# A graph network on one core: reordering the first chunks and the last blocks of a hand-written schedule

## The chip, the core and the metric

The kernel runs on one core of a Trainium2 chip. The core has five engines that run side by side, each through its own list of instructions in order: TensorE (PE, matrix products; its weight loads are a second row, PEld), VectorE (DVE), ScalarE (ACT), GpSimd (POOL) and SyncE (SP), which here only issues DMAs. The metric is the device time of one execution in microseconds (us), as the median of several runs.

## The reference

There are 128 graphs of 64 nodes with 128 features (`x`), and an adjacency matrix per graph (`adj`), ones on the diagonal and about one further entry in eight. One layer of message passing is computed:

```
pair[i, j]  = concat(x[i], x[j])
message     = mlp(pair; msg weights)                 # for each pair i, j
agg[i]      = sum over j of adj[i, j] * message[i, j]
out[i]      = x[i] + mlp(concat(x[i], agg[i]); upd weights)

mlp(v): h = layernorm(relu(v @ w0 + b0)) ; h = layernorm(relu(h @ w1 + b1)) ; h @ w2 + b2
```

All is float32. Messages are needed only where `adj` is one, so the kernel computes only those edges.

## The kernel before, in words

**Tiles.** Two graphs make a pair p (64 pairs), and each graph's edges fill at most 640 slots. Two pairs make a quad q (32 quads), which is 20 tiles of 128 edges. Four tiles are a chunk (160 chunks, five to a quad). Four pairs make a block b of nodes (16 blocks, ten chunks each).

**The way of an edge chunk.** For each pair, a table of one-hot columns `S` selects for every edge slot its two node rows; POOL, ACT and DVE build its halves (`node_rows`, `marks`, `compare`), and SP's DMAs stack them (`stack`). `rows` multiplies the turned `x` with the two halves of the first weight, `rows_hi` (ACT) and `rows_lo` (DVE) take the PSUM bank out as a high and a low part (`abh`, `abl`). `layer0` (L535) multiplies these with `S` into bank `hps` and ACT makes `h` (L538). `stats0` turns `h` on PE (L544) and DVE takes its statistics (L548). `var0_of` makes the variance of a quad (five operations on POOL; for the last quad on DVE), `root_of` its root on ACT (L255), split into a high and a low part (L562, L563), `turn_root` (L568) and `root_out` turn it into rows (`sdT`). `layer1` multiplies `h` with the centred second weight (L605), after a product of `sdT` with the bias table `b1t` (L602) or after ACT has seeded the bank (`seed`, L593); ACT makes `y` (L608), `stats1` its statistics on DVE (L615). `var1_step`, `root1_of` and `inverse_of` make one over the second deviation, `weights` (L678) scales a one-hot of destinations by it, and `reduce` (L691) sums the edges into nodes on PE: 20 products for two pairs, the scatter of a quad.

**The node update.** For each block, `Unit` holds the chain: `sums_out` copies the scatter's bank, `turn`, `turn_out` and `layer` go through three products, with relu and statistics on DVE (`layer_out`), variance, root, `upd_shift`, and `finish` (L791), which scales, adds the residual `xo` (POOL, L730) and issues the output DMA. `bias0` (DVE, L724) makes `m0`, the bias of its first product. The last block is split in two units of two pairs.

**The order.** Nothing is scheduled by a planner. Each step is entered by hand in `plan` under a chunk number and a place with `at(n, place, function, ...)`. For each chunk n the loop at the end runs the places in this order: `a`, `m`, layer 1 of chunk n - 8, `b`, layer 0, statistics 0, `k`, statistics 1, then `x`, `x1`, `x2`, `e0`, `e1`, `e`. A step's instructions go to their engines in that order, and an engine that waits holds all that stands behind it. PSUM has eight banks, each in a pool of one buffer: `mu` (`ubank`), `ma` (`abank`), `mk`, `hps`, `hT`, two `z`, `ys`.

**The head.** The steps for the first three chunks are written out ahead of the loop, with `keep_busy(k)`, which issues k products of a constant into a bank that nothing reads. During chunks 1 to 10 the loop also derives weights (`derivation`: products such as L180 in bank `mu` or a `z` bank, emptied by ACT or DVE), and `bias_table` and `bias_part` make `b1t` on POOL (L645 to L655). `odd_weights` (L427, L428) checks on DVE that `adj` holds only zeros and ones.

## Time and profile before

| | |
|---|---|
| median of 6 runs | 572.17 us (570.7 to 574.49) |
| the profiled execution, its own time | 572.43 us |
| its span | 570.7 us |
| PE busy | 549.1 us (96%) |
| DVE busy | 482.9 us (85%) |
| ACT busy | 480.8 us (84%) |
| POOL busy | 353.1 us (62%) |
| mean granted clock of PE | 0.989 |

The profile is one execution. Its span is counted from the first to the last instruction; the time of the execution is 1.73 us more. Busy times are sums over the whole span and say little about a stage: PE is busy through the body, so the edges of the span are read in windows of a few us and in the timeline. "PEclk" is the clock that PE was granted, 1.00 being full speed. In a timeline row the bracket gives how long the engine had been idle before, and which instruction ended that; a row with x4 merges four instructions that follow one another.

### The profile page before, as it was taken

To read this page: it belongs to the slowest core of one execution; us is meant where nothing else is said; L and a number is where in the kernel's file an instruction comes from. 1 tells how busy PE (TensorE), PEld (TensorE's weight loads), DVE (VectorE), ACT (ScalarE), POOL (GpSimd) and SP (SyncE) were. 2 spreads that over 40 slices of the span, in tenths; PEclk is the share of its full clock that TensorE was granted. 3 is DMA by queue.
4 is the path that set the end of the run, shared out by engine and by line. 5 is a ranking of instruction groups with operands and counts; after the bars stand their busy time and mean duration, and the time that the engine had idled before them with its cause. 6 is when DMAs were issued, how large, how long until landed. Compare 5 with 4: busy or idle time off the path is not lost. (4 is left out here: it accounts for less than half of the span.)

```text
span 570.7 us, 15800 instructions
## 1 busy us (share of the span) xinstructions
PE 549.1 (96%) x5325; PEld 514.8 (90%) x5325; DVE 482.9 (85%) x1944; ACT 480.8 (84%) x1153; POOL 353.1 (62%) x911
## 2 busy tenths in 40 slices
PE   8799899999999999999999999999999999989894
PEld 7587889999999999999999999999999999979883
DVE  6758788998989899898989899898989989885685
ACT  6778889998989899898989989898989989885533
POOL 3624566766757676675767676675767666545452
PEclk9889999999999999999999999999999999998999
DMA  4454747454564645655556545647454546432101
GB/s 103 121 127 114 136 104 132 107 132 109 107 155 105 142 92 143 112 118 127 126 130 113 141 108 132 106 111 153 112 143 84 131 113 108 113 94 28 39 20 42
DMA packets 90770, 63.23 MB, mean 111 GB/s; under 512 B 57398, under 2 KB 74812, under 8 KB 90684
## 3 DMA queue, kind: packets, MB, share of 16 engines
q1 hardware_dynamic: 90396, 62.03, 49.3%
q8 instruction: 44, 0.72, 0.6%
q14 instruction: 42, 0.34, 0.2%
q10 hardware_dynamic: 288, 0.13, 0.1%
HBM read 6.82 MB, written 4.19 MB: 19 GB/s over the span
## 5 line engine op out<-in xcount | busy, mean ns | idle before, releaser
L605 PE MATMUL z<-w1c,h 128*128 128x128 f32 x1280 | 172.8, 278 | 0.0
L548 DVE BATCH_NORM_STATS2 st<-hT 128x6 f32<-128x128 f32 x640 | 140.9, 282 | 32.1 <-PE hT L544 32.0
L605 PEld LDWEIGHTS z<-w1c,h 128*128 128x128 f32 x1280 | 161.0, 192 | 7.6 <-issue 5.1
L593 ACT ACTIVATE z<-b1b,m_sd 128x128 f32<-128x128 f32 x416 | 154.3, 371 | 10.4
L615 DVE BATCH_NORM_STATS2 st<-y 128x6 f32<-128x128 f32 x640 | 137.5, 277 | 2.8 <-ACT y L608 1.4
L608 ACT ACTIVATE y<-z 128x512 f32<-128x512 f32 x160 | 94.3, 590 | 22.3 <-PE z L605 20.6
L538 ACT ACTIVATE h<-hps,b0c 128x512 f32<-128x512 f32 x160 | 109.3, 683 | 2.2 <-PE hps L535 2.2
L544 PE MATMUL hT<-ident,h 128*128 128x128 f32 x640 | 97.9, 276 | 1.8 <-DVE st L548 1.6
L678 POOL TENSOR_TENSOR w<-oh,m_q 128x320 f32<-128x320 f16 x126 | 92.1, 743 | 9.9 <-PE hT L544 5.3
L535 PE MATMUL hps<-s,abl 128*128 128x512 f32 (+3 forms) x256 | 92.2, 372 | 2.0 <-ACT h L538 1.5
L544 PEld LDWEIGHTS hT<-ident,h 128*128 128x128 f32 x640 | 75.4, 141 | 13.9 <-DVE st L548 4.6
L535 PE MATMUL hps<-s,abh 128*128 128x512 f32 (+3 forms) x256 | 78.7, 326 | 0.0
L691 PE MATMUL ys<-y,w 128*64 128x128 f32 x1280 | 76.9, 275 | 0.0
L691 PEld LDWEIGHTS ys<-y,w 128*64 128x64 f32 x1280 | 69.2, 137 | 4.2 <-issue 3.6
L245 POOL TENSOR_TENSOR m_d<-st 128x20 f32<-128x20 f32 x62 | 16.4, 265 | 80.7 <-DVE st L548 69.0
L517 DVE TENSOR_TENSOR j<-mk,cmpt 128x320 fp32r<-128x320 f32 x124 | 58.7, 474 | 1.5 <-PE mk L509 1.5
L493 POOL CAST i<-tp 128x640 fp32r<-128x640 f16 x58 | 41.7, 719 | 25.2 <-ACT y L608 9.0
L478 ACT ACTIVATE d<-slot,mid 128x640 f16<-128x640 f16 x64 | 52.8, 824 | 0.0
L535 PEld LDWEIGHTS hps<-s,abl 128*128 128x128 f32 x256 | 49.3, 193 | 3.4 <-ACT h L538 2.3
L535 PEld LDWEIGHTS hps<-s,abh 128*128 128x128 f32 x256 | 49.5, 193 | 0.0
L469 DVE TENSOR_TENSOR abl<-mu,abh 128x512 fp32r<-128x512 f32 (+1 forms) x33 | 22.0, 668 | 30.3 <-ACT abh L463 30.2
L509 PE MATMUL mk<-tp,posall 128*128 128x320 f16 x126 | 38.0, 302 | 0.1
(227 smaller groups left out, 980.5 us busy)
## 6 DMA issues: line engine op xcount, KB each, us to landing
s<-i SPq DMA_DIRECT2D x124, 160.0 KB, 2.6
s<-j SPq DMA_DIRECT2D x124, 160.0 KB, 2.6
xn<-in_x_dram SPq DMA_DIRECT2D x15, 256.0 KB, 3.7
out_dram<-uo SPq DMA_DIRECT2D x15, 256.0 KB, 2.4
an<-in_adj_dram SPq DMA_DIRECT2D x16, 128.0 KB, 2.7
oh<-tp SPq DMA_TRANSPOSE x64, 3.4
xn<-in_x_dram SPq DMA_DIRECT2D x2, 128.0 KB
out_dram<-uo SPq DMA_DIRECT2D x2, 128.0 KB, 2.7
```

The costliest lines, as they stand in the source:

```text
L478: nc.scalar.activation(D[p], slot, AF.Abs, bias=blocks[b]["mid"][:, q:q + 1], scale=-1.0)
L517: nc.vector.tensor_tensor(JR[p][:, c], MK.pop((p, k))[:, 0:HC], cmpt[:, c], op=ALU.is_equal)
L535: nc.tensor.matmul(ps[:, c:c + w], lhsT=ab[:, g % 4, :], rhs=s, start=(k == 0), stop=(k == 1))
L538: nc.scalar.activation(H[n], ps, AF.Relu, bias=b0c)
L544: nc.tensor.transpose(ps[:, t, :], H[n][:, t * P:(t + 1) * P], ident)
L548: nc.vector.bn_stats(ST0[q][:, CH * c + t, :], ps[:, t, :])
L593: nc.scalar.activation(Z[n][:, t, :], W["b1b"], AF.Copy, scale=SR[q][:, k:k + 1])
L605: nc.tensor.matmul(ps[:, t, :], lhsT=h[:, t * P:(t + 1) * P], rhs=W["w1c"], start=False, stop=True, skip_group_check=True)
L608: nc.scalar.activation(Y[n], ps, AF.Relu)
L615: nc.vector.bn_stats(ST1[q][:, CH * c + t, :], Y[n][:, t, :])
L678: (nc.vector if p == NP - 2 else nc.gpsimd).tensor_tensor(WT[p][:, :, g, :], OH[p][:, :, g * N:(g + 1) * N], Q[q][:, k:k + TG].unsqueeze(2 ...
L691: nc.tensor.matmul(YS[b][g * N:(g + 1) * N, k, :], lhsT=w[:, t, g, :], rhs=y, start=(t == 0), stop=(t == TG - 1))
```

## The change

In the head, quad 0's variance moves in the order so that it stands ahead of `bias_table` on POOL. The rows of the second half of block 0 get bank `ma` in place of `mu`. Nine products of `keep_busy` are added at chunks 2 to 5. One cast and one distance (`node_rows(4)`, `distance(5)`) move behind the relu of their chunk on ACT. `odd_weights(0)` moves from chunk 18 to chunk 9. The first tiles of `adj` and `x` come from the pools that the later blocks use, and the loads of `adj` are issued six chunks later.

At the end, quad 31's variance (`var0_of`) runs in a new place `s`, ahead of layer 1 of its chunk, and the root and its turn one step earlier; the split of the root (L563) goes from DVE to POOL. The variances on DVE take one operation fewer, and two fewer where the first variance is folded in. The scatter of quad 29, the third last, goes from chunk 162 to chunk 167, behind the last layer 1; the copy of its sums follows it; quad 30's scatter takes bank `mk`. The buffers of `y` go from 12 to 15. `bias0` and `residual` of the last block come earlier, `finish` of block 13 later.

```diff
+    blkp = ctx.enter_context(tc.tile_pool(name="blk", bufs=3))
+    an0 = [blkp.tile([P, PB, N], F32, name="an", bufs=3) for b in range(2)]
+    xn0 = [blkp.tile([P, PB, C], F32, name="xn", bufs=5) for b in range(2)]
...
-    def square_sum(stp, st, n, name, eng=nc.gpsimd):
+    def square_sum(stp, st, n, name, eng=nc.gpsimd, m20=None):
...
-        eng.tensor_tensor(d, d, d, op=ALU.mult)
-        eng.tensor_scalar(d, d, C / 4.0, None, op0=ALU.mult)
+        if eng is nc.vector:
+            if m20 is not None:
+                eng.scalar_tensor_tensor(s, m20, EPS, s, op0=ALU.mult, op1=ALU.add)
+            eng.scalar_tensor_tensor(d, d, C / 4.0, d, op0=ALU.mult, op1=ALU.mult)
+        else:
+            eng.tensor_tensor(d, d, d, op=ALU.mult)
+            eng.tensor_scalar(d, d, C / 4.0, None, op0=ALU.mult)
...
     def var1_of(stp, st, m20, n, name, eng=nc.gpsimd):
+        if eng is nc.vector:
+            return square_sum(stp, st, n, name, eng, m20)
...
-        yp = es.enter_context(tc.tile_pool(name="yp", bufs=12))
+        yp = es.enter_context(tc.tile_pool(name="yp", bufs=15))
...
-            ps = blk["ab_ps", half] if k0 else ubank()
+            ps = blk["ab_ps", half] if k0 else abank() if (b, half) == (0, 1) else ubank()
...
-            eng_of(q).tensor_tensor(SH[q][:, 2:4, :], sdb, SH[q][:, 0:2, :].bitcast(F32),
+            nc.gpsimd.tensor_tensor(SH[q][:, 2:4, :], sdb, SH[q][:, 0:2, :].bitcast(F32),
...
-            if k == 0 or (b == NB - 1 and k == PB // 2):
+            if b == NB - 1 and k == 0:
+                YS[b] = ps_k.tile([P, 512], F32, name="mk").rearrange("p (k c) -> p k c", k=PB)
+            elif k == 0 or (b == NB - 1 and k == PB // 2):
                 YS[b] = ps_y.tile([P, PB, C], F32, name="ys")
...
-        LAST = ((1, 2, 3, 3, 4, 5, 6, 6, 8, 9, 10, 11, 11, 11, 12),
-                (0, 5, 6, 6, 7, 7, 8, 8, 8, 9, 9, 10, 10, 10, 11),
+        LAST = ((1, 2, 3, 3, 4, 5, 6, 6, 8, 9, 10, 11, 12, 11, 15),
+                (5, 5, 6, 6, 7, 7, 8, 8, 8, 9, 9, 10, 10, 10, 11),
...
-                at(max(o - 25, 0), "a", load_adj, b)
+                at(max(o - 19, 0), "a", load_adj, b)
...
-            for the last block: NCHK + L1 + 1, LAST[3], 1, 1 and NCHK + L1 - 1, LAST[2], 3, 3
+            for the last block: NCHK + L1 + 1, LAST[3], -5, 1 and NCHK + L1 - 1, LAST[2], -4, 3
-                at(n + m0_at, "m", bias0, u)
+                at(n + m0_at, "e" if b == NB - 1 else "m", bias0, u)
-                at(n + t[14], "m", finish, u)
+                at(n + t[14], "e" if b == NB - 3 else "m", finish, u)
...
-                    at(max(n - 7, p - 2), "a", distance, p)
+                    at(max(n - 7, p - 2), "x" if p == PB + 1 else "a", distance, p)
-                at(n - 5, "a", node_rows, p)
+                at(n - 5, "x" if p == PB else "a", node_rows, p)
...
-                wait = h + 2 if q == NQ - 3 else h + 1 if q == NQ - 2 else 2 + (2 * h + g + 1) // 2
+                wait = 3 if q == NQ - 3 else 2 if q == NQ - 2 else 2 + (2 * h + g + 1) // 2
-            at(NCHK + L1 + 1 if last else q * QC + SC - (q >= NQ - 3), "x1", reduce, p)
+            at(*((NCHK + L1 - 1, "x") if q == NQ - 3 else
+                 (NCHK + L1 + 1 if last else q * QC + SC - (q == NQ - 2), "x1")), reduce, p)
...
-            at(n, "e0", var0_of, q)
-            at(*((n, "e1") if last else (n + 1, "b")), root_of, q)
-            at(*((n + 2, "b") if last else (n + 1 if q else QC + 1, "x")), turn_root, q)
-            at(n + 2 if q else QC + 2, "x" if last else "a", root_out, q)
+            at(3 if q == 0 else n, "s" if last else "x" if q == 0 else "e0", var0_of, q)
+            at(*((n, "e0") if last else (n + 1, "b")), root_of, q)
+            at(*((n + 1, "x1") if last else (n + 1 if q else QC + 1, "x")), turn_root, q)
+            at(n + 2 if q else QC + 2, "a", root_out, q)
-            wait = 0 if last else 1 if q == NQ - 2 else 2
-            at(end + wait, "a", root1_of, q)
-            at(end + wait, "m", inverse_of, q)
+            wait = 0 if last else 2
+            at(end + wait, "x" if q == NQ - 2 else "a", root1_of, q)
+            at(end + wait, "x" if q == NQ - 2 else "m", inverse_of, q)
...
-        at(18, "m", odd_weights, 0)
+        at(9, "m", odd_weights, 0)
-        at(3, "b", bias_table)
+        at(3, "e", bias_table)
+        for n, k in ((2, 2), (3, 3), (4, 2), (5, 2)):
+            at(n, "e", keep_busy, k)
...
+            run(n, "s")
             if 0 <= n - L1 < NCHK:
                 layer1(n - L1)
```

The two lines on the last block's units stand for two longer lines in which only those numbers change.

## The prediction

> **What bounds the kernel now.** I read the page's slices first, then the busy time of short windows where they dip, then the timeline there.

> ```profile
> PE   8799899999999999999999999999999999989894
> PEclk9889999999999999999999999999999999998999
> ```

> TensorE (PE) is at nine tenths or more from about 60 to 510 us, so the body is PE's own work. Only the two ends, which the change edits, can give time back. The chain of waits is of no use here (two instructions), so I follow the timeline. Windows of the head (columns: length, busy us and count of PE, PEld, DVE, ACT, POOL, then granted clock, DMA share, GB/s):

> ```profile
> 22.00:24.00 2.00, 0.59 (x9) 0.35 (x6) 1.27 (x4) 0.58 (x1) 1.92 (x6) 1.00 0.67 163
> 24.00:26.00 2.00, 2.00 (x10) 1.33 (x10) 0.53 (x3) 1.15 (x4) 1.15 (x5) 0.82 0.73 176
> 26.00:28.00 2.00, 0.87 (x5) 0.58 (x4) 1.91 (x3) 2.00 (x6) 2.00 (x2) 0.50 0.27 60
> 30.00:32.00 2.00, 2.00 (x9) 1.57 (x7) 1.28 (x5) 1.22 (x4) 1.19 (x2) 0.50 0.02 4
> 32.00:34.00 2.00, 2.00 (x16) 1.78 (x15) 0.68 (x4) 1.06 (x3) 0.00 (x0) 0.98 0.68 163
> ```

> PE idles 1.4 us, and then runs at half clock: from 25.3 us (0.82 over 2 us is 0.72 us at half) to 32.1 us, 6.8 us in all. The timeline of the head (start, length, what; in brackets the idle time before it and who ended it):

> ```profile
> 22.93 0.45 POOL L649 TENSOR_TENSOR b1mix<-b1mix,b1lo 128x128 f32<-128x128 f32 x1
> 23.06 0.69 DVE L469 TENSOR_TENSOR abl<-mu,abh 128x512 fp32r<-128x512 f32 x1 [0.72 <-ACT abh L463]
> 23.35 0.25 POOL L245 TENSOR_TENSOR m_d<-st 128x20 f32<-128x20 f32 x1
> 23.81 0.49 PE L180 MATMUL mu<-wg,mean_m 128*128 128x128 f32 x2 [1.41 <-DVE abl L469]
> 24.82 0.31 ACT L255 ACTIVATE m_sd<-m,eps_c 128x20 f32<-128x20 f32 x1 [1.79 <-POOL m L249]
> 27.09 0.68 ACT L538 ACTIVATE h<-hps,b0c 128x512 f32<-128x512 f32 x1
> 27.82 0.48 PE L535 MATMUL hps<-s,abl 128*128 128x128 f32 x1 [1.13 <-ACT h L538]
> ```

> Two waits. A weight product (L180) needs bank mu, which the rows of the second half hold until DVE has emptied it. And ACT's root (L255) waits for POOL, whose variance stands behind the bias table's four operations; the relu of chunk 5 (L538) is queued behind that root, a cast and a distance, and PE waits for it.

> The end:

> ```profile
> 534.70 0.31 ACT L255 ACTIVATE m_sd<-m,eps_c 128x20 f32<-128x20 f32 x1 [2.13 <-DVE m L249]
> 535.56 0.31 PE L568 MATMUL ma<-ident,sh 128*80 128x128 f32 x1 [0.48 <-DVE sh L563]
> 535.80 2.40 PE L691 MATMUL ys<-y,w 128*64 128x128 f32 x40
> 538.13 0.51 PE L602 MATMUL z<-b1t,sdT 80*128 80x512 f32 x1
> 550.19 2.54 DVE L724 SCALAR_TENSOR_TENSOR m<-c2u,deg,ub0b 128x128 f32<-128x128 f32 x4
> 551.05 2.40 PE L691 MATMUL ys<-y,w 128*64 128x128 f32 x40
> 553.50 0.37 ACT L717 COPY ysum<-ys 128x256 f32<-128x256 f32 x1 [4.26 <-PE ys L691]
> 565.09 0.30 ACT L269 ACTIVATE um_sq<-um_v,eps_c 128x2 f32<-128x2 f32 x1 [1.90 <-DVE um_v L263]
> ```

> PE is nearly full up to the last scatter (551.05), and from 553.5 a serial chain through all engines ends the kernel.

> **The change, head.** The fillers: 2 matmuls after chunk 2, 3 and 2 around the weight products, 2 after chunk 5. A pair like L180's takes about 0.22 us of PE per product (products start 23.81 and 24.13, rows of the trace), so nine cost 2.0 us where PE has work, nothing where it waits. The first two delay chunk 3's transposes (20.36), hence everything after, by 0.35. The second-half rows then end near 22.6. With their own bank, 3 fillers (0.66), the products (0.22 + 0.32 + 0.4) and 2 fillers (0.44) bring chunk 5's layer 0 to 24.55, where it was 24.86; abl is ready at 24.1. So the bank and its fillers gain 0.3 us here, and close the gap that preceded the clock's fall.

> The variance is 1.44 us of POOL (23.35 to 24.79). Ahead of the table it starts when the fourth chunk's statistics are done, near 22.4, and the root runs at 23.85. ACT also takes the relu of chunk 5 ahead of the cast (0.71) and the distance (0.82): the relu runs at 25.45, when its matmuls end, and PE's next layer 0 at 26.45 (after 2 fillers) instead of 27.82. Late next is ACT: cast, distance, two copies end at 28.2, for which the product w2u waits; two products (0.9) later chunk 7 starts at 29.1, before 32.10. DVE agrees: its tp takes 1.09 beside POOL's table (before too), the statistics of chunk 5 end at 29.95, and chunk 6's transposes start there, 0.25 after PE could. Gain 2.8 us, of which about 1.8 is the clock (4.3 us of PE work from 27.8 to 32.1 at half). The table is later by the variance: its first part ends near 27.5, its first reader starts at 31.7, so 4 us of cover.

> [...] The trace has it fall behind gaps of 1.4 us (22 us) and 1.9 us (510 us), and not behind 1.47 us at 58.5. [...] The measured row decides: 2.8.

> The second adjacency check (L427 and L428, 0.41 + 0.42 us of DVE) moves from 64 us, where DVE is full but PE idles only 0.14 us in two, to chunk 9, where DVE had 0.27 and 0.24 us idle between statistics. It costs 0.3 (0 to 0.5).

> Free: adj loads move six chunks down SP's queue, behind some ten stack copies and transposes of 0.6 to 1.3 us issue each, and keep five chunks (some 17 us) against 2.7 us to land; SP gets no DMA more, and the stacks that now go ahead land no later; the pooled first tiles wait for no reader that is late; y's 15 buffers only let the moved scatter read late. The steady state is untouched.

> **The change, end.** Quad 31's variance goes ahead of layer 1's statistics, four operations of 0.18 instead of five on DVE; it ends near 532.7, so the root runs then instead of at 534.70. Its split moves to POOL, ahead of four weight operations, which start at 533.6 instead of 531.2; their reader is now 9 us later. The turn is on PE at 533.9 without a wait, and sdT at 534.6 is in time for its first reader at 535.1.

> The scatter of quad 29 (2.16 us of issue) leaves 535.80 and runs behind the last layer 1. PE does the same work up to the last scatter, 20.7 us from 530.57; before it ended at 553.2, so 1.9 us was idle. After, I keep 0.6 (the copies ysum and ysumT that PE waits for, 0.52 before). Gain 1.3: the last ysum at 552.2. m0 leaves 550.19: four take 1.12 us undisturbed (row at 503.42), 2.54 beside POOL's xo, so between statistics they cost 1.1 to 2.5 us of DVE, which has that much idle from 538 to 545. uo of block 13 (1.1 us) takes their place, in front of a wait for PE; its output DMA leaves SP near 548 instead of 544, long before the last at 567. Quad 30's root comes one chunk later: its weights end on POOL near 544.6 (2.77 us for four), its scatter starts near 544.7, so there is no slack, and each 0.1 us late is 0.1 lost. The last block's variances lose one and two DVE operations on the final chain (0.16 to 0.2 each): 0.5. End: 1.8 us (0.5 to 2.3).

> Sum: 2.8 - 0.3 + 1.8 = 4.3 us. The profiled execution took 572.43, 0.26 above the median of 572.17; less 4.3 that is 568.1, and I say 568.0.

> **Rivals.**
> First: the fall of the clock is not what fillers prevent, or most runs did not have it. Then the head gives 1.0, the whole 2.5, time 569.8. Against it: the profiled run, with the fall, is at the median. 16%.
> Second: the end gains nothing, as the moved scatter pushes the last one by what the turn saves (PE then waits for ysum as long as it idled). Head alone: 2.5 us, 569.8. For it: the same PE work; against it: the root is 2 us earlier. 10%.
> Third, slower: the clock falls in the head in spite of the fillers and stays down for two spans of 3.4 us more, the fillers then being work at half rate. Nine cost 4.0 us, the longer half clock 3.4, while bank and relu give back 2.5 of waits and the other items 1.5, net 3.4: 575.8. It decides only if PE still idles over 1.4 us in one stretch between 21 and 27 us; I find 0.3 there. 4%.
> Fourth, better: the gap at 510 us falls elsewhere in the clock's rhythm and its 3.4 us at half clock (1.7 us lost) go too: 566. 10%.
> Main case: 60%, own range 566 to 570.

> **Numbers.** Under 0.3% (1.7 us) this kernel's measurement can't tell a change from none. Faster by more needs 570.4 or less: the main case, the fourth, and most of the first two: 0.84. Same: both small cases together: 0.11. Slower: 0.05. Range 564.8 to 571.0.

> **What would show it.** Right: no gap over 0.5 us on PE from 22 to 28, clock 1.00 there, chunk 7 some 3 us earlier; the root near 23.9; the two scatters (ys, mk) together after the last layer 1 near 542 to 547 of before's count, and the last ysum 1.3 us earlier than the head explains. Wrong: half clock at 25 us again, first layer 1 waiting for b1t, or PE idle over 1 us between mk and the last ysum.

## The result

| | before | after |
|---|---|---|
| median | 571.99 us (570.66 to 574.93, 39 runs) | 570.07 us (567.81 to 571.38, 18 runs) |
| the profiled execution | 572.43 us | 569.85 us |
| its span | 570.7 us | 568.0 us |
| mean granted clock of PE | 0.989 | 0.995 |

The ratio is 0.9963, with a 95% interval of 0.9952 to 0.9975: faster by 1.92 us in the medians and by 2.58 us between the two profiles. The forecast was 4.3 us. In the two profiles the head with the body gave 2.4 us where the sum had 2.5, and the end gave 0.3 us, a sixth of its 1.8.

In the page of after, the slices with the head are back at 9 in PEclk, and the slice near 510 us keeps its 8:

```profile
PE   8998999999999999999999999999999999989994
PEclk9999999999999999999999999999999999998999
```

The head in windows of 2 us (columns as before: length, busy us and count of PE, PEld, DVE, ACT, POOL, granted clock, DMA share, GB/s). PE no longer has the hole at 22 us, and the granted clock is 1.00 in every row:

```profile
22.00:24.00 2.00, 2.00 (x26) 1.76 (x25) 1.27 (x6) 0.58 (x1) 0.98 (x5) 1.00 0.58 146
24.00:26.00 2.00, 2.00 (x15) 1.49 (x14) 1.21 (x4) 1.09 (x4) 1.81 (x5) 1.00 0.70 168
26.00:28.00 2.00, 2.00 (x17) 1.92 (x16) 1.09 (x2) 1.97 (x4) 2.00 (x3) 1.00 0.00 0
30.00:32.00 2.00, 1.91 (x16) 1.58 (x14) 1.64 (x8) 1.52 (x6) 2.00 (x3) 1.00 0.14 30
```

The timeline of the head shows the two steps of the change at work: the fillers (L926; x6 are three of them, two instructions each) run where PE idled, and ACT's root stands at 24.19 instead of 24.82, the relu of chunk 5 at 26.03 instead of 27.09. Chunk 7's layer 0, at 32.10 before, starts at 29.51:

```profile
23.09 0.94 PE L926 MATMUL ys<-mean_m 128*128 128x128 f32 x6
24.19 0.31 ACT L261 ACTIVATE m_sd<-m,eps_c 128x20 f32<-128x20 f32 x1 [0.39 <-POOL m L255]
26.03 0.69 ACT L545 ACTIVATE h<-hps,b0c 128x512 f32<-128x512 f32 x1 [0.43 <-PE hps L542]
26.31 0.61 PE L926 MATMUL ys<-mean_m 128*128 128x128 f32 x4
26.77 0.33 PE L542 MATMUL hps<-s,abl 128*128 128x128 f32 x1
29.51 0.39 PE L542 MATMUL hps<-s,abl 128*128 128x256 f32 x1
```

The timeline of the end. The early root is there (530.45, before 534.70), the moved scatter of quad 29 too (539.94). But POOL starts the weights of quad 30 only at 541.35, PE's next scatter (`mk`) stops after its first product (the row with x2), and the last sums stand at 551.37:

```profile
530.45 0.31 ACT L261 ACTIVATE m_sd<-m,eps_c 128x20 f32<-128x20 f32 x1
539.94 2.40 PE L700 MATMUL ys<-y,w 128*64 128x128 f32 x40
541.35 2.86 POOL L685 TENSOR_TENSOR w<-oh,m_q 128x320 f32<-128x320 f16 x4 [3.43 <-PE ys L700]
542.18 0.38 PE L700 MATMUL mk<-y,w 128*64 128x128 f32 x2
542.87 2.70 PE L700 MATMUL mk<-y,w 128*64 128x128 f32 x38 [0.31 <-POOL w L685]
545.50 0.66 PE L745 MATMUL ma<-ident,ysum 128*128 128x128 f32 x4
548.92 2.40 PE L700 MATMUL ys<-y,w 128*64 128x128 f32 x40
551.37 0.37 ACT L726 COPY ysum<-ys 128x256 f32<-128x256 f32 x1 [4.26 <-PE ys L700]
```

I split every profile at the same points: the relus of chunks 0, 8 and 159, the last copy of `ysum`, the last `uo`. The first stretch is the head and body, without the start of the program, which varies (the relu of chunk 0 came between 9.35 and 11.85 us).

| profile | chunk 0 to 8 | chunk 0 to 159 | to last `ysum` | to last `uo` |
|---|---|---|---|---|
| before | 26.64 | 519.01 | 24.76 | 12.00 |
| after | 24.12 | 516.62 | 24.78 | 11.69 |

So 2.39 us come from the head and body (2.52 up to chunk 8), nothing from the end up to the last sums, and 0.31 from the final chain. These numbers are used below for each experiment.

The runs of a kernel also fall into groups by the mean granted clock. In the 57 runs of before that stood beside the experiments, 29 had a clock of 0.992 or less (median 572.35) and 28 had 0.994 or 0.995 (median 570.88); none had more. Of 20 runs of after, 10 had 0.994 or 0.995 (median 570.19) and 10 had 0.996 to 0.998 (median 568.9; three of them lie at 570.5 to 571.4, which I can't explain). The two profiles suggest what the groups are in the main: ahead of the final chain, the profile of before has two stretches at half clock, 6.8 us from 25.27 and 3.4 us from 513.38 us, and a mean of 0.989; that of after has only one, 3.4 us from 511.22 us, and 0.995. (Both have a further stretch at half clock behind the last `uo`, from 567.99 us in before and 565.83 in after, where PE has no matmul left. It costs no time that shows, but lowers the mean by 0.002, so the mean alone does not count the falls.) At the same mean, 0.994 or 0.995, after is 0.69 us faster; the rest of its gain is in its runs at 0.996 and more, which before does not have.

### The profile page after: what moved, and what is told of

It is laid out like the page before. It is cut to its first block, busy times and chain, and to the rows that moved or that the text cites. A ratio compares the mean times of both kernels' runs of the same rounds, so it can differ in the third digit from the quotient of the medians.

```text
span 568.0 us, 15829 instructions
## 1 busy us (share of the span) xinstructions
PE 549.4 (97%) x5343; PEld 515.5 (91%) x5343; DVE 480.8 (85%) x1937; ACT 481.2 (85%) x1153; POOL 352.9 (62%) x912
## 5 line engine op out<-in xcount | busy, mean ns | idle before, releaser
L700 PE MATMUL ys<-y,w 128*64 128x128 f32 x1240 | 74.5, 275 | 0.0
L700 PEld LDWEIGHTS ys<-y,w 128*64 128x64 f32 x1240 | 67.0, 137 | 4.1 <-issue 3.6
L476 DVE TENSOR_TENSOR abl<-mu,abh 128x512 fp32r<-128x512 f32 (+1 forms) x32 | 21.4, 668 | 29.2 <-ACT abh L470 29.1
```

The source lines that it names most:

```text
L700: nc.tensor.matmul(YS[b][g * N:(g + 1) * N, k, :], lhsT=w[:, t, g, :], rhs=y, start=(t == 0), stop=(t == TG - 1))
```

## Experiments on the head

Diffs are against the changed kernel where nothing else is said. Line numbers of the changed kernel and of the experiments are up to 14 above those of before.

**The head alone.** The changed kernel with the end of before (its variances, scatter, `LAST`, banks), keeping the pooled first tiles. The diff of this one is against before.

```diff
-        at(18, "m", odd_weights, 0)
+        at(9, "m", odd_weights, 0)
-        at(3, "b", bias_table)
+        at(3, "e", bias_table)
+        for n, k in ((2, 2), (3, 3), (4, 2), (5, 2)):
+            at(n, "e", keep_busy, k)
...
-            ps = blk["ab_ps", half] if k0 else ubank()
+            ps = blk["ab_ps", half] if k0 else abank() if (b, half) == (0, 1) else ubank()
```

> The head of the change (variance ahead of the table, own bank, fillers, the two ACT steps, the adjacency check, the pooled first tiles) with the end of before. If all the gain is made in the head and the end gives only its shorter final chain: chunk 7 and the whole body 2.1 to 2.4 us earlier than before, span 568.3 to 568.8, that is about 0.3 to 0.6 us longer than the changed kernel's 568.0. If the end gave as much as was forecast (1.8 us) the span would be near 569.8, with the body as early.

Measured: 569.89 us (568.03 to 570.59, 14 runs), ratio 0.9965 (0.9953 to 0.9977), against 0.9963 for the whole change. Its profile has 24.13 from chunk 0 to 8 and 516.68 to chunk 159, as after has. Five runs at clock 0.998 took 568.0 to 568.3, nine at 0.994 or 0.995 took 569.8 to 570.6. The head is the gain, but for the final chain: from the last `ysum` to the last `uo` it takes 11.98, against 11.69 in after.

**Without the fillers.** The changed kernel without its nine products of `keep_busy`.

```diff
-        for n, k in ((2, 2), (3, 3), (4, 2), (5, 2)):
-            at(n, "e", keep_busy, k)
```

> The changed kernel without the nine filler products of chunks 2 to 5. If the fillers hold the clock: TensorE idles about 1 us near 23 and again near 26, half clock follows from 25 us for one or two spans of 3.4 us in part of the runs, and the body is 0.5 to 1.5 us later than in the changed kernel. If the clock would have stayed up (the gaps are now under 1 us each): full clock, and the body 0.4 to 0.9 us earlier, since the first fillers delay the statistics of chunk 4 by 0.43 us.

Measured: 567.62 us (567.02 to 568.88, 6 runs), ratio 0.9933 (0.9918 to 0.9948), so 2.4 us below after in the medians. From chunk 0 to 8 it takes 22.76, 1.36 less than after: that is what the nine fillers cost. The rest of the 2.4 is clock: five of these six runs have a mean of 0.996 or more, half of those of after. At 0.996 and more the medians are 567.5 and 568.9, which again is 1.4. The windows of its head show a granted clock of 1.00 without them, with gaps of 0.36 us or less:

```profile
22.00:24.00 2.00, 1.64 (x14) 1.12 (x9) 1.27 (x4) 1.12 (x3) 1.73 (x7) 1.00 0.68 164
24.00:26.00 2.00, 1.75 (x10) 1.18 (x9) 1.38 (x4) 1.87 (x5) 1.92 (x4) 1.00 0.35 92
26.00:28.00 2.00, 1.83 (x13) 1.36 (x11) 1.35 (x5) 2.00 (x6) 2.00 (x3) 1.00 0.48 119
```

**The fillers alone, in the kernel before.**

```diff
         at(3, "b", bias_table)
+        for n, k in ((2, 2), (3, 3), (4, 2), (5, 2)):
+            at(n, "e", keep_busy, k)
```

> The kernel before, with the nine filler matmuls added and nothing else. If fillers hold the clock where the two waits of the head are still there: half clock in the head is gone or halved, and the time is 0 to 1.5 us below the kernel before. If they only take PE's time (1.4 us for nine in the changed kernel, by the run without them): the gap ahead of the weight products stays, since the fillers stand ahead of it or behind it and not in it, half clock comes as before, and the time is 1.4 to 2 us above the kernel before (fillers at half clock cost twice).

Measured: 568.66 us (568.27 to 570.91, 9 runs), ratio 0.9955 (0.9939 to 0.9971): within the intervals as much as the whole change brings, from two lines. Seven of nine runs have clock 0.998. The granted clock is 1.00 from 18 to 34 us in this profile, and from 506 to 518 too, where the gap near 510 us is there as before (1.92 us); so this profile is also without the fall near 510 us, with the gap in front of it unchanged. The expectation's second theory fails: in the timeline the three fillers of chunk 3 stand in the hole ahead of the weight product, and cut it from 1.41 us to 0.55; those of chunk 5 cut the wait for the relu from 1.13 to 0.20:

```profile
22.69 0.94 PE L916 MATMUL ys<-mean_m 128*128 128x128 f32 x6
24.17 0.49 PE L180 MATMUL mu<-wg,mean_m 128*128 128x128 f32 x2 [0.55 <-DVE abl L469]
27.54 0.33 PE L535 MATMUL hps<-s,abl 128*128 128x128 f32 x1 [0.20 <-ACT h L538]
```

From chunk 0 to 8 it takes 24.53. So the head stands at a clock of 1.00 with the fillers alone, as it does with the two new orders alone (22 to 28 us, above). Where the gaps are, fillers cost nothing that shows (24.53, against 24.73 for the same order at full clock without them, in the run with the end alone below); where the orders have closed the gaps, as in after, the fillers only cost.

**One order at a time, without fillers.** First with the second half's rows back in bank `mu`, then with the variance back behind the bias table.

```diff
-            ps = blk["ab_ps", half] if k0 else abank() if (b, half) == (0, 1) else ubank()
+            ps = blk["ab_ps", half] if k0 else ubank()
```

> The changed kernel without the nine fillers, and with the rows of the second half of block 0 back in bank mu (the variance still ahead of the bias table). Theory A (the bank is what keeps PE fed: with it the weight products lie under the statistics of the third chunk): PE idles 1 us or more again between 21 and 24 us, the granted clock falls in part of the runs, the body is 1 us or more later than without the fillers alone (568.9 in its profile, median 567.6), so near 569. Theory B (the order of the variance is worth all of the head, the bank nothing): within 0.4 us of the kernel that lacks the fillers alone, so 567.3 to 568.

```diff
-            at(3 if q == 0 else n, "s" if last else "x" if q == 0 else "e0", var0_of, q)
+            at(n, "s" if last else "e0", var0_of, q)
-        at(3, "e", bias_table)
+        at(3, "b", bias_table)
```

> The changed kernel without the nine fillers, and with the variance of the first quad back behind the bias table, as in the kernel before (the own bank stays). Theory B (the order is worth all): ACT's root is back near 24.8 us, the relu of chunk 5 waits for it behind POOL, PE idles over 1 us ahead of chunk 6, the body starts 2 us or more later than without the fillers alone: 569.5 to 571. Theory A (the bank and the full clock are worth it): the relu is late by 1 us, but without half clock that is all that is lost: 568.3 to 569.0.

Measured: with `mu` 568.38 us (568.16 to 569.61, 6 runs), ratio 0.9947 (0.9927 to 0.9966), 24.41 from chunk 0 to 8; with the old variance 568.74 us (567.55 to 571.12, 9 runs), 0.9953 (0.9933 to 0.9972), 24.72. Against 22.76 with both orders they lose 1.65 and 1.96 us in the head. Both keep the cast and the distance behind the relu on ACT, whose own share no run shows. In both profiles one stretch of 3.4 us at half clock is back, from 25.10 us with `mu` and from 25.88 us with the old variance, by their windows of 1 us. With `mu` it follows the 1.41 us gap; with the old variance it follows two short ones, of 0.36 and 0.92. The timeline's gap and the window after it, with `mu`:

```profile
23.64 0.49 PE L181 MATMUL mu<-wg,mean_m 128*128 128x128 f32 x2 [1.41 <-DVE abl L476]
```

```profile
26.00:28.00 2.00, 2.00 (x9) 1.76 (x9) 1.56 (x3) 2.00 (x6) 2.00 (x2) 0.50 0.00 0
```

and with the old variance:

```profile
25.67 0.64 PE L181 MATMUL z<-wg,mean_m 128*128 128x128 f32 x2 [0.92 <-ACT wg L178]
```

```profile
26.00:28.00 2.00, 1.90 (x8) 1.50 (x8) 0.27 (x1) 2.00 (x6) 2.00 (x3) 0.50 0.00 0
```

Neither theory holds alone: bank and variance are worth about the same, and each without the other left a fall in its profile. By the medians they lose less, 0.8 and 1.1 us. With the old variance, two runs at clock 0.998 took 567.6 and 567.7, the other seven 568.0 to 571.1. With `mu`, two runs at 0.997 took 568.2 and 568.4, no less than the profiled one with its fall (568.19), so what that fall adds to the time is not shown there.

**The check of `adj`.** The combined kernel (below) with the second check of block 0 back at chunk 18.

```diff
-        at(9, "m", odd_weights, 0)
+        at(18, "m", odd_weights, 0)
```

> The combined kernel (no fillers, weights' own buffers, early uo of block 13, early ysumT) with the second adjacency check of block 0 back at chunk 18, where it was before the change. If its place at chunk 9 costs what was forecast (0.3 us of the body between chunks 8 and 20): chunk 20 stands 0.3 us earlier against the kernel's own start than in the combined kernel (which ran 564.36), and the time is 564.1. If DVE had the room at chunk 9: no difference over 0.1 us at chunk 20, and 564.2 to 564.7.

Measured: 566.09 us (564.72 to 566.25, 6 runs), ratio 0.9897 (0.9881 to 0.9913), 1.7 us slower than the combined kernel and not faster. The timeline shows 0.7 of it. The first tiles now come from the pool of three that the later blocks use, and block 0's tile is read by its check until 61.7 us. The load of `adj` for block 3 waits in SP's queue from 37 us to 46.78, until a check that stands at chunk 13 (46.31), of another block, has read its tile, and the stacks behind it come late for PE:

```profile
35.70 1.31 SPq L677 DMA_TRANSPOSE oh<-tp  x1
46.31 0.41 DVE L434 SCALAR_TENSOR_TENSOR a<-an 128x256 f32<-128x256 f32 x1
46.78 0.39 SPq L347 DMA_DIRECT2D an<-in_adj_dram  x1
49.20 1.23 SPq L507 DMA_DIRECT2D s<-j  x2
...
52.15 0.47 PE L542 MATMUL hps<-s,abl 128*128 128x512 f32 x1 [1.56 <-DMA s<-j]
```

From chunk 8 to 20 this profile takes 36.50, the combined kernel's 35.80. The other 1.0 us of the medians is not in the profile; five of the six runs have a clock of 0.994 to 0.996, but whether the clock fell behind the new gap of 1.56 us is not shown. The move to chunk 9 is thus not an extra but what the pooled tiles need. The price of both together is read from chunk 8 to 20: 35.66 in before, 35.81 in after, 0.15 us.

## Experiments on the end

**The end alone.** The changed kernel with the head of before, keeping the pooled tiles, with the check at chunk 18.

```diff
-            ps = blk["ab_ps", half] if k0 else abank() if (b, half) == (0, 1) else ubank()
+            ps = blk["ab_ps", half] if k0 else ubank()
...
-        at(9, "m", odd_weights, 0)
+        at(18, "m", odd_weights, 0)
-        at(3, "e", bias_table)
-        for n, k in ((2, 2), (3, 3), (4, 2), (5, 2)):
-            at(n, "e", keep_busy, k)
+        at(3, "b", bias_table)
```

and the orders on ACT and the variance of quad 0 as in before.

> The end of the change with the head of before (the pooled first tiles stay, since 15 buffers of y need their room). If a new wait at quad 30's weights eats what the earlier turn saves: last ysum where before has it within 0.3 us, span 0.3 to 0.6 us under before's. If the end works and the loss is somewhere else: 1.5 us or more under before's. The half clock at 25 us stays in both.

Measured: 571.58 us (569.76 to 576.11, 14 runs, with clocks from 0.981 to 0.998), ratio 1.0012 (0.9995 to 1.0029). Part of that comes from the experiment's own edit: with the check at chunk 18 it has the queue wait just shown (PE waits 1.45 us for a stack at 54.30, and chunks 12 to 16 take 12.48 instead of 11.75). Less that 0.7, it is at before. In its profile the end takes 24.77 to the last `ysum`, as before and after, and 11.67 from there to the last `uo`. The end gives 0.3 us, all in the final chain.

This profile (569.76 us, the fastest of the 14) also has no stretch at half clock in the head or at 511 us (granted clock 1.00 from 22 to 32 and from 506 to 518 us), though the gaps of before are all there, 1.41, 1.59 and 1.91 us. The timeline's gaps and the windows behind them:

```profile
24.30 0.49 PE L181 MATMUL mu<-wg,mean_m 128*128 128x128 f32 x2 [1.41 <-DVE abl L476]
28.31 0.33 PE L542 MATMUL hps<-s,abl 128*128 128x128 f32 x1 [1.59 <-ACT h L545]
```

```profile
24.00:26.00 2.00, 1.70 (x9) 1.20 (x10) 1.02 (x4) 0.67 (x3) 1.15 (x6) 1.00 0.66 159
26.00:28.00 2.00, 0.72 (x5) 0.38 (x4) 1.73 (x3) 2.00 (x5) 2.00 (x3) 1.00 0.05 13
```

Its 24.73 from chunk 0 to 8 is the head of before at full clock, 1.91 less than in the profile of before.

**Buffers of their own for quad 30's weights.** They take buffers of the edge tables, which are no longer needed, and not the two buffers of `w`.

```diff
-                WT[p] = wp.tile([P, TG, 2, N], F32, name="w")
+                if q == NQ - 2:
+                    WT[p] = sp.tile([P, 2, CAP], F32R, name="s").bitcast(F32).rearrange(
+                        "p a c -> p (a c)")[:, 0:TG * 2 * N].rearrange(
+                        "p (t g n) -> p t g n", t=TG, g=2)
+                else:
+                    WT[p] = wp.tile([P, TG, 2, N], F32, name="w")
```

> The changed kernel, with the two weight tiles of quad 30 in buffers of the edge tables, which nothing uses by then, so that they do not wait for the scatter of quad 29. If that wait is what took the end's gain: quad 30's weights start on POOL near 539.5 instead of 541.35, its scatter runs its 2.4 us without a stall instead of 3.4, the last ysum is 1.0 to 1.2 us earlier, span 566.8 to 567.0. If TensorE's own work bounds the end, or the copies of the sums do, under 0.3 us.

Measured: 567.81 us (567.39 to 570.08, 7 runs), ratio 0.9951 (0.9934 to 0.9968). The median gain over after is one of the clock, as far as the profile shows (0.998 and no fall), since the end still takes 24.71. The timeline shows the first wait gone and a second in its place: the scatter `mk` is whole, but the layer of block 14 then waits 0.80 us for bank `mu`, which block 13's moved `finish` has not emptied; on DVE that stands behind two weight operations of quad 31.

```profile
537.27 2.77 POOL L690 TENSOR_TENSOR s<-oh,m_q 128x320 f32<-128x320 f16 x4 [1.64 <-DVE m_q L282]
539.88 2.35 PE L705 MATMUL mk<-y,s 128*64 128x128 f32 x40
541.56 1.93 DVE L690 TENSOR_TENSOR w<-oh,m_q 128x320 f32<-128x320 f16 x2 [0.20 <-DVE m_q L282]
543.41 1.11 DVE L805 SCALAR_TENSOR_TENSOR uo<-mu,um_q,xo 128x128 f32<-128x128 f32 x4
544.58 0.49 PE L764 MATMUL mu<-u0a,xnT 128*128 128x128 f32 x2 [0.80 <-DVE uo L805]
```

**And block 13's `finish` back at its place**, on top of the weights' own buffers.

```diff
-        LAST = ((1, 2, 3, 3, 4, 5, 6, 6, 8, 9, 10, 11, 12, 11, 15),
+        LAST = ((1, 2, 3, 3, 4, 5, 6, 6, 8, 9, 10, 11, 12, 11, 12),
-                at(n + t[14], "e" if b == NB - 3 else "m", finish, u)
+                at(n + t[14], "m", finish, u)
```

> The changed kernel, with quad 30's weights in buffers of their own (so that they do not wait for the moved scatter) and with the last operation of block 13 (uo, which empties bank mu) one phase and three chunks earlier, where the kernel before had it. If the end gained nothing because of these two waits in a row, the last ysum now comes 1.0 to 1.5 us sooner after the last layer 1 than in the changed kernel, the final chain stays at 11.7, and the time at the same clock is 1.0 to 1.5 us lower: 568.5 to 569.0 where the clock falls once, 566.7 to 567.3 where it does not. If PE's work sets the end anyway (the rival), the last ysum stays where it was after the last layer 1, and the time within 0.3 us of the kernel that has the weights' buffers alone at the same clock.

Measured: 567.85 us (566.90 to 568.90, 6 runs), ratio 0.9930 (0.9908 to 0.9953): three runs at clock 0.996 with 566.9 to 567.0, three at 0.993 with 568.7 to 568.9, as the first theory has it. Now the end takes 23.74 to the last `ysum`, 1.04 less than after, and 11.69 from there, as after. Both waits are gone from its timeline:

```profile
540.03 2.77 POOL L690 TENSOR_TENSOR s<-oh,m_q 128x320 f32<-128x320 f16 x4 [2.21 <-DVE m_q L282]
542.07 2.35 PE L705 MATMUL mk<-y,s 128*64 128x128 f32 x40
545.80 0.39 PE L764 MATMUL mu<-u0a,xnT 128*128 128x128 f32 x2
550.23 0.37 ACT L731 COPY ysum<-ys 128x256 f32<-128x256 f32 x1 [4.26 <-PE ys L705]
```

**`ysumT` of block 13 ahead of the seeds.** The gap of 1.91 us near 510 us is in before and after alike. It is ACT's order: four seeds, 1.59 us together, stand ahead of the copy that PE waits for.

```diff
-                at(n + t[2], "a", turn_out, u, "ysum")
+                at(*((n + t[1], "x") if b == NB - 3 else (n + t[2], "a")), turn_out, u, "ysum")
```

> The changed kernel, and of block 13 the turned sums (ysumT) are copied out of bank ma right behind their transposes, ahead of the four seeds that ACT ran first near 508 us. If the gap at 508 us is that order on ACT: PE's idle time there falls from 1.9 us to 0.5 or less, the clock no longer falls there, and every run is in the group at clock 0.998; body shorter by 1.2 us against runs without the fall and by 2.9 us against runs with it: 566.5 to 567.5. If the gap has another cause behind it (the layer's operands, DVE): it stays above 1 us, and times split in two groups as in the changed kernel, 567.8 and 570.

Measured: 567.34 us (566.48 to 569.88, 6 runs), ratio 0.9923 (0.9905 to 0.9941), clock 0.996 to 0.998 in every run. The gap shrinks to 0.68 us, not to the 0.5 expected, and the granted clock is 1.00 from 506 to 520 us. In the timeline of after the gap reads

```profile
510.41 0.66 PE L745 MATMUL ma<-ident,uy 128*128 128x128 f32 x4 [1.91 <-ACT ysumT L750]
```

and here

```profile
511.21 0.66 PE L745 MATMUL ma<-ident,uy 128*128 128x128 f32 x4 [0.68 <-ACT ysumT L750]
```

To chunk 159 it takes 513.94, 2.68 less than after: 1.0 without a fall in either (e.g. 514.95 with the weights' own buffers), the rest the fall. (This profile began 1.9 us later than that of after, and is the slowest of the six.)

**All together.** No fillers, the weights' own buffers, `finish` back, `ysumT` early.

```diff
-        for n, k in ((2, 2), (3, 3), (4, 2), (5, 2)):
-            at(n, "e", keep_busy, k)
+                if q == NQ - 2:
+                    WT[p] = sp.tile([P, 2, CAP], F32R, name="s").bitcast(F32).rearrange(
...
-                at(n + t[2], "a", turn_out, u, "ysum")
+                at(*((n + t[1], "x") if b == NB - 3 else (n + t[2], "a")), turn_out, u, "ysum")
-                at(n + t[14], "e" if b == NB - 3 else "m", finish, u)
+                at(n + t[14], "m", finish, u)
```

> All pieces that looked good at once: the changed kernel without fillers, with the weights' own buffers, the early uo of block 13, and the turned sums of block 13 (ysumT) copied right behind their transposes, ahead of the seeds that ACT ran first at 508 us. If the pieces add: 2.4 us below the changed kernel for the fillers, 1.0 to 1.5 for the end, and 1 to 1.7 more in runs in which the clock no longer falls at 510 us: 565.5 to 567. If the gap at 510 only moves, or the end does not follow: 567.2 to 568.

Measured: 564.36 us (564.15 to 565.16, 4 runs), ratio 0.9870 (0.9846 to 0.9895): it beats both kernels. Its profile has 22.81 from chunk 0 to 8, 512.52 to chunk 159, 23.74 to the last `ysum` and 11.68 from there. The pieces add, to 1.1 us more than the 565.5 to 567 expected.

**The scatter of quad 29 back, in the combined kernel.**

```diff
-            at(*((NCHK + L1 - 1, "x") if q == NQ - 3 else
-                 (NCHK + L1 + 1 if last else q * QC + SC - (q == NQ - 2), "x1")), reduce, p)
+            at(NCHK + L1 + 1 if last else q * QC + SC - (q >= NQ - 3), "x1", reduce, p)
```

(and the weights of quad 29 at their old chunks)

> The combined kernel with the scatter of quad 29 back where it was before the change, ahead of the last layer-1 chunks. If the moved scatter is what filled PE's idle time at the end: PE idles about 1 us more between the last layer 1 and the last scatter (waiting for the weights of quad 30), the last ysum comes 1 us later than in the combined kernel, 565.4. If the early root and turn of quad 31 did it and the place of the scatter is indifferent: within 0.3 us, 564.1 to 564.7. If the moved scatter was itself a loss: 563.5 to 564.

Measured: 567.27 us (566.69 to 567.62, 6 runs), ratio 0.9919 (0.9904 to 0.9934); the end takes 26.06, 2.3 us more than with the scatter moved. The first theory holds, at twice its size. Quad 30's root is one chunk later than in before, POOL's weights start at 538.86, and without the moved scatter PE has nothing to do while they are made:

```profile
538.86 2.77 POOL L690 TENSOR_TENSOR s<-oh,m_q 128x320 f32<-128x320 f16 x4 [5.07 <-DVE m_q L282]
539.63 0.43 PE L705 MATMUL mk<-y,s 128*64 128x128 f32 x2 [0.90 <-POOL s L690]
540.31 2.67 PE L705 MATMUL mk<-y,s 128*64 128x128 f32 x38 [0.25 <-POOL s L690]
```

The moved scatter is the right step. It needs the weights behind it to have buffers.

## Why the prediction was right or wrong

The median, 570.07, lies at the outer edge of the main case (566 to 570) and next to the 569.8 of the first two rivals. The direction was right, and so was the head as a place of gain; the size was less than half of the forecast (1.92 of 4.3), since the end failed and the clock gave less.

**The head, 2.8 us: nearly right in the profiles, with a wrong part.** Chunk 0 to 8 went from 26.64 to 24.12, 2.52 us. Its parts can be put together from profiles at full clock: before's head with its fall 26.64, without it 24.73 (1.91 us of clock, forecast 1.8); both orders without fillers 22.76 (1.97 us of waits); fillers back, 24.12 (1.36 us lost). (The run without the fall has before's order in the head with the pooled tiles.) Waits less fillers are 0.61 where I had 1.0. The nine fillers stand 2.25 us on PE from start to start (0.55, 0.77, 0.47 and 0.46), 0.25 each where I had 0.22; some 0.9 of that lies in waits that PE has without them. (My terms behind 22.6 also sum to 24.64 and not to 24.55.) The root (23.85 forecast, 24.19 measured) and chunk 7's layer 0 (29.1 forecast, 29.51) came where the steps put them, given a start that was 0.24 us later.

**The fillers: their role was wrong.** I took them as what keeps the clock up and costed them as needed. The run without them has a clock of 1.00 in the head and is 1.36 us shorter there; the run with them alone is, within the intervals, as fast as the whole change. The step that failed is "the bank and its fillers gain 0.3 us here, and close the gap that preceded the clock's fall": the bank cuts that gap from 1.41 to 0.36 us without them, and with the variance's new place no fall is left in the profile. With the fillers alone the clock was 1.00 there too.

**The check, -0.3: the sign right, the size half (0.15, with the pooled tiles).** Under "Free" I wrote that the pooled tiles wait for no reader that is late. That holds only because the check moved; the two lines belong together, which I had not seen.

**The end, 1.8 us: wrong, 0.3 measured.** The final chain gave 0.31 (forecast 0.5). The 1.3 us up to the last sums did not come. The second rival's time did (569.8 forecast, 569.85 in the profile), but by another wait than it named, and the first rival gives the same time. The step that failed is "its weights end on POOL near 544.6 (2.77 us for four), its scatter starts near 544.7, so there is no slack". I had timed quad 30's weights by their scale (`m_q`, ready at 539.5 in after) and not by their buffers: `w` has two, and the moved scatter of quad 29 held them, the first until 541.3. `mk` then took 3.32 us from its start to the next transposes, where the combined kernel takes 2.28: 1.04 us, all of the difference between 24.78 and 23.74. With buffers of their own the forecast of 1.3 is nearly met, but only with `finish` back too. Of that move I said that it stands "in front of a wait for PE"; its price is a second wait behind the first, 0.80 us for bank `mu`, that the first one hid. In two other profiles (the one without fillers and the one with `ysumT` early) both waits show, and the end takes 25.60.

**The slices.** That PE is "at nine tenths or more from about 60 to 510 us" misread two digits: the slices from 57 to 71 us and from 499 to 514 us stand at 8. So it was not true that only the two ends could give time back: in the second of these, `ysumT` ahead of the seeds took 1.0 us out of the body, and no fall came behind the 0.68 us left.

**The clock, rivals one and four.** I gave the fall in the head to every run of before. By their mean clock, half of its runs had less half clock than the profile, though where it is missing in them no profile shows. So the median gain (1.92) is smaller than the gain between profiles (2.58). Rival four, a missing fall at 511 us, came in about half of the runs of after, if the ten of 20 at 0.996 and more are those without it.

## What to carry to other kernels

When work is moved behind other work, follow the buffers of what comes next as well as its data: a pool of two holds its next writer until the moved reader is done (`w` here, until 541.3 us), and the wait behind that one is seen only when the first is gone. Try fillers and a better order apart before they are put in together; where the order closes the gap, a filler is only work (1.36 us for nine here). A gap on PE can be worth more than its length: behind the one of 1.91 us the clock fell in five of the ten profiles that have it, at 1.7 us a fall, though it did not behind those of 1.47 us at 58.5 us in before and 1.46 us at 56.4 us in after. So look at groups of runs by their clock before a median is explained.

## What the runs showed that I had not expected

- A fall came with no single gap over 1 us ahead of it (0.36 and 0.92 us, with the old variance; clock 0.50 from 26 to 29 us). One fall at 511 us costs 1.67 us (to chunk 159, 516.62 in after and 514.95 with the weights' own buffers, the same up to there otherwise).
- Some of DVE's small operations were longer while POOL worked. In after's end, the five operations of quad 31's second variance took 0.53, 0.18, 0.59, 0.17 and 0.59 us beside POOL's weights, where such operations take 0.16 to 0.20 in the end of before with POOL idle. Two weight operations on DVE took 0.89 in after, with POOL idle, and 1.93 with the weights' own buffers, with POOL at its own weights. `finish` stands behind these operations: the end of after has no wait for bank `mu`; that of the kernel without fillers, where the same two took 1.46 us, part of it beside POOL's, has 0.75 us, with the same order.
